# Four graph layers on one core: a mask and a product moved from VectorE to GpSimd, with other prices in the instruction planner

## The chip, the cores and the metric

The kernel runs on one core of one Trainium2 chip. The metric is the device time of one execution in microseconds (us); smaller is better. TensorE (PE in the profile; PEld is its weight load) multiplies matrices, VectorE (DVE) and ScalarE (ACT) work on tiles elementwise, GpSimd (POOL) can too, and SyncE (SP) issues most of the transfers (DMAs).

## The reference

There are 16 batches of 1024 nodes with 128 features, and for each batch a sparse adjacency matrix of 1024 x 1024. Four layers follow each other; each begins with a layer norm and a maximum with 0, and its result is added to its input.

```python
h = relu(layernorm(x)); x = x + L0(h, adj, adj, W, b)    # mean over neighbours, linear
h = relu(layernorm(x)); x = x + L1(h, adj, W, b)         # normalised adjacency, linear
h = relu(layernorm(x)); x = x + L2(h, adj, ...)          # two rounds of edge scores and messages
h = relu(layernorm(x)); x = x + L3(h, adj, W, a)         # attention
# L2, per round l: a score for each pair of nodes
hid    = relu(a[:, :, None, :] + b[:, None, :, :] + be1[l])
scores = sigmoid(hid @ We2[l] + be2[l])
messages = (adjacency * scores) @ x
# L3
e = (Wh1 + swapaxes(Wh2, 1, 2)) * A_                     # A_ = A + identity
e = where(e >= 0, e, ALPHA * e)
attention = softmax(where(A_ > 0, e, NEG_INF))
h_prime = attention @ Wh
```

## The kernel before, in words

The 1024 nodes of a batch are 8 blocks of 128. Layer 2 needs scores only where the adjacency matrix has an entry. For each pair of blocks the kernel builds one-hot matrices (`st`, `om`, `omT`, `onT`) from the matrix; matmuls with them pick the features of the two ends of each edge into slots (`pre`, L1343 and L1349), VectorE and ScalarE make the hidden values from them (`hid`, L1364 and L1365), and matmuls with a column of signs add them up to scores (L1389). Pairs of blocks are handled in nine groups: two of blocks on the diagonal, which have one direction, and seven off the diagonal, which have two directions, `d` 0 and 1. There are two rounds, `l` 0 and 1.

In `scores`, the scores of a group (`tan`) become `u`, two 16-bit halves in one 32-bit word (L1422, L1423; L1429 copies some rows to other partitions). Then `u` is multiplied with the one-hots `onT` into `val` (L1441): one instruction of 128 x 1024 for each direction of an off-diagonal group, two for a diagonal group. `scatter` spreads `val` over the matrix of the pair of blocks with matmuls (L1486). Those of direction 1 write only 64 rows of PSUM, since they use 64 columns of weights; they are called narrow below. The result is multiplied with the adjacency matrix (`upd`, L1493) and gives the messages (L439).

Layer 3 is in `Lane.layer3`. Its rows of output are taken in three parts (3, 3 and 2 blocks), and each part in four steps of two blocks `k`. A step loads a strip of the transposed adjacency matrix (`at`; it has one buffer, except in the last batch), adds the identity where it belongs (L764), makes the products `e` (L765, two instructions), the leaky maximum (L769), the exponential on ScalarE (L770), and multiplies by the mask "adjacency above 0" (L771: comparison and product in one instruction). Then TensorE adds up `e` times `wh` (the `hp` matmuls of L439). There are 12 steps in a batch, 192 in all.

GpSimd does only the powers of the layer norms (L496, eight in a batch, 128 in all) and a few set-up instructions.

Batches are interleaved: while layer 2 of one batch runs, layer 3 of the batch before and layers 0 and 1 of the next one, with the building of its one-hots, run beside it. Python generators first write down all instructions in a rough order (`weave`, with shares of time in `MAIN_US`, `FIRST_US`, `LAST_US`). Then the class `Issue` sets the order on every engine: it gives each instruction a price (`costs`), walks the graph of dependences forwards and backwards as a list scheduler with the number of buffers in mind (`walk`), and does so `PASSES` times; the plan with the earliest last start is written into the program as a fixed order for each engine's queue. So a price in `costs` changes no instruction, only the order. Every engine then works through its queue in that order, and an instruction that waits holds up what stands behind it.

The prices that matter below: `SWITCH_NS` is charged when TensorE goes from fp32 to 16-bit matmuls or from narrow to wide ones; a GpSimd instruction costs a flat 1560 ns.

Of the kernel before, what the change touches and what calls it, by code (L numbers as in the profile page):

```python
# [10 lines left out]
F32 = mybir.dt.float32  # L11
# [4 lines left out]
OP = mybir.AluOpType  # L16
# [41 lines left out]

SIGNAL_NS = 45.0
RESULT_NS = {"PE": 163.0, "Activation": 120.0, "DVE": 88.0, "Pool": 80.0}  # L60
SWITCH_NS = 60.0
DMA_NS, DMA_NS_PER_BYTE, DMA_NS_BEHIND, DMAS = 1900.0, 3.9e-3, 3.3e-3, 8
PASSES = 3


class Issue:
# [63 lines left out]
    def costs(self):  # L130


        self.busy, self.late, self.form, self.bytes = [], [], [], []
        for op, queue, kind in zip(self.ops, self.queue, self.kind):
            out, form = op.outs[0].bass_ap, (False, False)
            n, late, size = self.size(op.outs[0]), RESULT_NS.get(queue, 0.0), 0
            aps = [a.bass_ap for a in op.ins if hasattr(a, "bass_ap")]
            psum = bool(aps) and aps[0].space == bass.MemoryType.PSUM
            if kind == "Matmult":
                n = self.size(op.ins[0])  # L140
                form = op.ins[0].dtype == F32, out.shape[0] < 128
                if form[0]:
                    busy = max(n / 1.2 + 6, 112) * (1 if op.is_transpose else 2)
                else:
                    busy = 32 if form[1] else max(n / 2.4 + 2.5, 25)
            elif kind == "DMACopy":
                size = n * WIDTH[op.outs[0].dtype] * out.shape[0]
                inside = all(a.space == bass.MemoryType.SB for a in (out, aps[0]))
                busy = 630 if inside else 470
                late = DMA_NS + size * DMA_NS_PER_BYTE - busy  # L150
            elif queue == "Activation":
                busy = n / 1.2 + (50 if psum else 92) + 92 * (len(aps) - 1)
            elif queue == "DVE":
                wide = [a for a in aps if a.size() > 128]
                fast = kind == "TensorScalarPtr" and len(wide) == 1 and not psum
                if kind in ("BNStats", "TensorReduce"):
                    n = self.size(op.ins[0])
                busy = n * (0.53 if fast else 1.0625) + 55 + 64 * (len(aps) > len(wide))
            else:
                busy = 1560  # L160
            self.bytes.append(size)
            self.busy.append(busy)
            self.late.append(busy + late)
            self.form.append(form)
# [24 lines left out]

    def switched(self, j, was, back):  # L190
        one, two = (self.form[j], was) if back else (was, self.form[j])
        return any(a and not b for a, b in zip(one, two))

    def walk(self, rank, seq, back=False):


        n, queues = len(self.ops), sorted(set(self.queue))
        edges, others = (self.front, self.after) if back else (self.after, self.front)
        waits = [len(v) for v in others]
        users, turn, homes = self.turns(seq)  # L200
        given, parked, live, over = dict.fromkeys(homes, 0), {}, {}, {}
        ready, start, line = [0.0] * n, [0.0] * n, {q: [] for q in queues}
        soon, now = {q: [] for q in queues}, {q: [] for q in queues}
        free, sent, was = dict.fromkeys(queues, 0.0), [(0.0, 0.0, 0)] * DMAS, (False, False)

        def offer(j):

            new = {}
            for name in self.uses[j]:
                if name in turn and name not in live:  # L210
                    new.setdefault(self.tiles[name].tag, set()).add(turn[name])
                else:
                    ready[j] = max(ready[j], live.get(name, 0.0))
            for tag, mine in new.items():
                at = given[tag]
                while at in mine:
                    at += 1
                if at <= max(mine) or len(homes[tag]) < len(mine):
                    key = at + 1 if at <= max(mine) else given[tag]
                    parked.setdefault((tag, key), []).append(j)  # L220
                    return
                ready[j] = max(ready[j], sorted(homes[tag])[len(mine) - 1])
            heappush(soon[self.queue[j]], (ready[j], rank[j], j))

        for j in range(n):
            if not waits[j]:
                offer(j)
        for _ in range(n):
            at, q = min(
                (free[q] if now[q] else max(free[q], soon[q][0][0]), q)  # L230
                for q in queues if now[q] or soon[q]
            )
            while soon[q] and soon[q][0][0] <= at:
                heappush(now[q], heappop(soon[q])[1:])
            j = heappop(now[q])[1]
            more = 0.0
            if self.kind[j] == "DMACopy" and not back:
                at = max(at, sent[0][1])
                more = DMA_NS_BEHIND * sum(
                    n * (end - at) / (end - then) for then, end, n in sent if end > at  # L240
                )
                sent = sent[1:] + [(at, at + self.late[j] + more, self.bytes[j])]
            elif q == "PE":
                at += SWITCH_NS * self.switched(j, was, back)
                was = self.form[j]
            start[j], free[q] = at, at + self.busy[j]
            line[q].append(j)
            end = at + (self.busy[j] if back else self.late[j] + more + SIGNAL_NS)
            freed = {}
            for name in self.uses[j]:  # L250
                users[name] -= 1
                over[name] = max(over.get(name, 0.0), end)
                if name not in turn:
                    continue
                tag = self.tiles[name].tag
                if name not in live:
                    live[name] = heappop(homes[tag])
                    freed.setdefault(tag, []).append(given[tag] + 1)
                    given[tag] += 1
                if not users[name]:  # L260
                    heappush(homes[tag], over[name])
                    freed.setdefault(tag, []).append(given[tag])
            for tag, keys in freed.items():
                for key in dict.fromkeys(keys):
                    for k in parked.pop((tag, key), ()):
                        offer(k)
            for k, lag in edges[j]:
                ready[k] = max(ready[k], at + lag + more * (lag > 0.0))
                waits[k] -= 1
                if not waits[k]:  # L270
                    offer(k)
        return start, line
# [26 lines left out]
def tile_four_gnn_layers(  # L299
# [22 lines left out]
    nc = tc.nc  # L322
# [45 lines left out]
    rows = {name: const.tile([P, L, D], F32, name=f"{name}_bc") for name in ("gamma", "beta")}  # L368
# [362 lines left out]
    class Lane(Layers):  # L731
# [5 lines left out]
        def layer3(self, xt, strip, name):  # L737
# [14 lines left out]
            for lo, hi in L3_ROWS:  # L752
                n = hi - lo
# [3 lines left out]
                for k in range(0, T, 2):  # L757
                    at = strip(k, lo, hi)
                    e = flat(self.scratch(f"e_{name}_{lo}_{k}"))[:, : 2 * n * P]
                    e = e.rearrange("p (k n) -> p k n", k=2)  # L760
                    for i in range(2):
                        if lo <= k + i < hi:
                            own = at[:, i, (k + i - lo) * P : (k + i + 1 - lo) * P]
                            nc.vector.tensor_add(own, own, ident)  # L764
                        nc.vector.scalar_tensor_tensor(  # L765
                            e[:, i], wh1[:, lo * P : hi * P], wh2[:, k + i : k + i + 1], at[:, i],
                            op0=OP.add, op1=OP.mult,
                        )
                    nc.vector.scalar_tensor_tensor(e, e, L3_ALPHA, e, op0=OP.mult, op1=OP.max)  # L769
                    nc.scalar.activation(e, e, AF.Exp)  # L770
                    nc.vector.scalar_tensor_tensor(e, at, 0.0, e, op0=OP.is_gt, op1=OP.mult)  # L771
                    yield 0.4 * n
                    for i in range(2):
                        for t in range(n):
# [22 lines left out]
    class Edges:  # L797
# [490 lines left out]
        class Group:  # L1288
# [126 lines left out]
            def scores(self):  # L1415


                path, name, rows = self.path, self.name, self.rows
# [15 lines left out]
                for d in range(nd):  # L1434
                    for i in range(0, Q, each):
# [2 lines left out]
                        )  # L1438
                        n = val.shape[-1]
                        v = u[:, :, i * nd + d : (i + each - 1) * nd + d + 1 : nd]  # L1440
                        nc.vector.tensor_tensor(  # L1441
                            val, onT[:, i : i + each].rearrange("p i (c n) -> p i c n", n=n),
                            v.rearrange("p k i o -> p i k o").to_broadcast([P, each, SEGMENTS, n]),
                            op=OP.mult,
# [370 lines left out]
```

## Time and profile before

| what | value |
|---|---|
| time, median of 3 runs | 4691.72 us (4684.89 to 4700.5) |
| the profiled execution's own time | 4697.63 us |
| its span in the profile | 4695.5 us |
| mean granted TensorE clock | 0.979 |
| instructions | 132226 |
| GpSimd: powers of 128 x 8 (64), median | 1.637 us |
| GpSimd: powers of 128 x 4 (64), median | 1.007 us |
| VectorE: L765, 128 x 384 (256) and 128 x 256 (128), mean | 0.615 and 0.482 us |
| VectorE: L769, 128 x 768 (128) and 128 x 512 (64), mean | 0.956 and 0.686 us |

The profile is of one execution. Busy time is the time in which an engine had an instruction in work, as a share of the span; durations of VectorE instructions that follow each other overlap by a little under 0.1 us in the records. A group of instructions is shown as line, engine, operation, output<-input, shapes and count, then its busy time in us and the mean of one in ns, then the idle time of the engine just before them and who ended it. The chain of work is followed back from the last instruction, at each step to what released it. Idle time of an engine that isn't the bottleneck costs nothing.

### The profile page before, as it was taken

The page shows a single profiled execution, that of the slowest core. Times are in us where ns is not written, and L with a number is a line of the kernel's source. Part 1 is how long each engine was busy: PE and PEld are TensorE (multiplying, and loading weights), DVE is VectorE, ACT ScalarE, POOL GpSimd, SP SyncE. Part 2 cuts the span into 40 slices and gives each one's busy share as a digit, 9 for nine tenths or more (in the row PEclk, how much of TensorE's full clock was granted, in tenths as well). Part 3 has the DMA queues.
Part 4 walks back from the last instruction along what each step waited for, and adds up shares of the span by engine and source line. Part 5 has one row for each costly group of instructions (what it writes and reads, how often), then busy time and mean ns, then how long its engine had stood idle before and what let it go on. Part 6 is the DMA issues. An engine that isn't in the chain of part 4 may idle for free.

```text
span 4695.5 us, 132226 instructions
## 1 busy us (share of the span) xinstructions
PE 4427.7 (94%) x53685; PEld 3608.7 (77%) x53685; DVE 3876.9 (83%) x9128; ACT 3003.4 (64%) x7238; POOL 187.0 (4%) x137
## 2 busy tenths in 40 slices
PE   6999999999999999999999999999999999999986
PEld 5777778777777777877777787777877777787765
DVE  4777797987969789797897979879797897979877
ACT  5666575675756667576675766757567575766643
POOL 0000000000000000000000000000000000000000
PEclk8999999999999999999999999999999999999997
DMA  7363635345363443635436353453634426344221
GB/s 211 82 179 81 188 89 162 108 121 169 86 183 107 132 142 86 190 106 148 118 88 203 88 160 114 120 170 87 184 102 135 143 83 192 104 140 126 80 79 56
DMA packets 852858, 603.42 MB, mean 129 GB/s; under 512 B 128528, under 2 KB 782608, under 8 KB 852240
## 3 DMA queue, kind: packets, MB, share of 16 engines
q1 hardware_dynamic: 847136, 593.24, 43.4%
q8 instruction: 423, 6.93, 0.6%
q10 hardware_dynamic: 5104, 1.65, 0.1%
q14 instruction: 195, 1.60, 0.1%
HBM read 446.44 MB, written 100.66 MB: 117 GB/s over the span
## 4 chain that ended last, share of the span: by engine, by line
PE 54%; DVE 29%; ACT 7%; DMA 6%; issue 2%; POOL 1%; SPq 0%; ACTq 0%; DVEq 0%; POOLq 0%
PE nb L543 7%; PE pre L1343 7%; PE p L1486 7%; DVE hid L1365 6%; PE msg L439 5%; DVE val L1441 5%; PE sc L1389 4%; PE h L597 4%; PE pre L1349 4%; DVE omT L1197 2%; PE xn L606 2%; PE bb L551 2%; PE tn L1038 2%; DMA both<-part 2%; DVE upd L1493 2%
## 5 line engine op out<-in xcount | busy, mean ns | idle before, releaser
L1364 ACT ACTIVATE hid<-pre 128x320 f16<-128x320 f32 (+1 forms) x2048 | 903.5, 460 | 330.5 <-PE pre L1349 316.2
L1365 DVE SCALAR_TENSOR_TENSOR hid<-pre,hid 128x320 f16<-128x320 f32 (+1 forms) x2048 | 998.5, 508 | 97.2 <-ACT hid L1364 88.7
L1343 PE MATMUL pre<-om,part 128*128 128x320 fp8e4 (+1 forms) x4096 | 960.8, 308 | 14.3 <-DVE hid L1365 6.5
L1441 DVE TENSOR_TENSOR val<-onT,u 128x1024 f32<-128x1024 fp8e4 x576 | 695.9, 1218 | 1.8
L1349 PE MATMUL pre<-st,both 128*128 128x176 fp8e4 (+1 forms) x4096 | 678.1, 243 | 18.3 <-DMA both<-part 17.3
L439 PE MATMUL msg<-upd,xf 128*128 128x128 f32 (+3 forms) x3008 | 663.2, 329 | 1.9 <-DVE upd L1493 1.7
L1349 PEld LDWEIGHTS <-both 128*128 128x128 f16 x4096 | 385.5, 98 | 172.7 <-issue 27.5
L439 PEld LDWEIGHTS msg<-upd,xf 128*128 128x128 f32 x3008 | 428.7, 191 | 29.3 <-issue 13.6
L1389 PE MATMUL sc<-slide,hid 128*128 128x1 f16 x12800 | 438.6, 163 | 10.7 <-DVE hid L1365 10.0
L1389 PEld LDWEIGHTS <-hid 128*128 128x128 f16 x12800 | 408.2, 96 | 52.7 <-DVE hid L1365 25.3
L1204 ACT ACTIVATE om<-pm 128x320 fp8e4<-128x320 f32 (+1 forms) x576 | 271.6, 472 | 197.4 <-PE pm L1150 191.2
L1486 PE MATMUL p<-val,omT 128*128 128x64 f16 (+1 forms) x6528 | 383.0, 204 | 14.9 <-DVE val L1441 10.9
L1343 PEld LDWEIGHTS <-part 128*128 128x128 f16 x4096 | 339.6, 98 | 69.8 <-issue 30.1
L1410 ACT ACTIVATE tan<-sc,be_s,down 128x8 f32<-128x8 f32 (+1 forms) x960 | 297.9, 357 | 133.7 <-PE sc L1389 128.8
L1493 DVE SCALAR_TENSOR_TENSOR upd<-p,adj 128x512 f32<-128x512 f32 x512 | 351.5, 687 | 31.5 <-PE p L1486 25.6
L1486 PEld LDWEIGHTS <-omT 128*128 128x128 fp8e4 x6528 | 333.8, 97 | 41.0 <-issue 20.0
L439 PE MATMUL hp<-wh,e 128*128 128x129 f32 x2048 | 332.9, 289 | 23.7 <-DVE e L771 18.1
L1189 ACT ACTIVATE onT<-pn 128x256 fp8e4<-128x256 f32 (+1 forms) x576 | 253.1, 440 | 112.1 <-PE pn L1135 101.9
L439 PEld LDWEIGHTS hp<-wh,e 128*128 128x128 f32 x2048 | 275.4, 196 | 33.4 <-DVE e L771 21.9
L1110 ACT ACTIVATE far<-iota_off,mid 128x384 f16<-128x384 f16 x448 | 271.0, 628 | 44.6 <-DVE st L1114 42.8
L1114 DVE TENSOR_SCALAR st<-far,wid 128x384 fp8e4<-128x384 f16 (+1 forms) x576 | 238.9, 428 | 70.3 <-PE pre L1349 34.3
L543 PEld LDWEIGHTS nb<-z,l 128*128 128x128 f32 x2048 | 255.8, 196 | 27.0 <-issue 12.9
(224 smaller groups left out, 7943.9 us busy)
## 6 DMA issues: line engine op xcount, KB each, us to landing
at<-in_adj_dram SPq DMA_DIRECT2D x128, 512.0 KB, 5.1
ct<-in_adj_dram SPq DMA_DIRECT2D x128, 512.0 KB, 5.0
adjT<-tn SPq DMA_DIRECT2D x128, 512.0 KB, 6.1
l<-adjT SPq DMA_DIRECT2D x128, 512.0 KB, 5.1
adj<-adjT SPq DMA_DIRECT2D x256, 256.0 KB, 3.5
a<-adjT SPq DMA_DIRECT2D x128, 384.0 KB, 3.9
both<-part SPq DMA_DIRECT2D x256, 128.0 KB, 3.4
adj<-adjT SPq DMA_DIRECT2D x448, 64.0 KB, 2.6
```

The costliest lines, as they stand in the source:

```text
L439: nc.tensor.matmul(dst, left, right, start=opened is None, stop=True, skip_group_check=True)
L543: nc.tensor.matmul(ps, mat[:, k], z[:, k], start=(k == 0), stop=(k == T - 1))
L1204: nc.scalar.activation(om, pm, AF.Copy, saturate=False)
L1343: nc.tensor.matmul(pre[:, :c], parts[:, k, u % Q, 1 - d], om, start=(k == 0), stop=True, skip_group_check=True,)
L1349: ins = nc.tensor.matmul(pre[:, at : at + n], both[:, k, t % Q, d], st[:, first : first + n], start=False, stop=True, skip_group_check=True,)
L1364: nc.scalar.activation(hid[:, 0, :c], pre[:, :c], AF.Relu)
L1365: nc.vector.scalar_tensor_tensor(hid[:, 1, :c], pre[:, :c], 0.0, hid[:, 0, :c], op0=OP.max, op1=OP.subtract)
L1389: nc.tensor.matmul(sc[:, k, g : g + 1], self.hid[self.done + g][:, v, at : at + P], sign, start=(g, v, k) == (*order[0], 0), stop=True, sk ...
L1410: nc.scalar.activation(dst, src, AF.Tanh, bias=path.be2[:, self.l : self.l + 1], scale=path.down[:, self.l : self.l + 1],)
L1441: nc.vector.tensor_tensor(val, onT[:, i : i + each].rearrange("p i (c n) -> p i c n", n=n), v.rearrange("p k i o -> p i k o").to_broadcast ...
L1486: nc.tensor.matmul(dst, left, right, start=n < first, stop=True, skip_group_check=True)
L1493: nc.vector.scalar_tensor_tensor(upd, ps, S_SCALE, self.adj[:, d * Q : (d + 1) * Q], op0=OP.add, op1=OP.mult,)
```

## The change

Layer 3's mask is made on GpSimd in two instructions, a comparison that overwrites the strip and a product after the exponential, in place of VectorE's one. In round `l` 1, the product of scores and one-hots for direction 1 is issued on GpSimd. In the planner the prices change: a switch between narrow and wide matmuls costs 94 or 119 ns and one between fp32 and 16-bit none; a narrow matmul 29 ns; GpSimd instructions of 64 elements or more per row go by their length, and the flat price stays for the rest; VectorE instructions whose output begins at another partition than their input cost 130 ns more, and every small operand counts. There are four passes, not three.

```diff
-SWITCH_NS = 60.0
+NARROW_NS, WIDE_NS, HELD_NS = 94.0, 119.0, 130.0
-PASSES = 3
+PASSES = 4
...
-            out, form = op.outs[0].bass_ap, (False, False)
+            out, form = op.outs[0].bass_ap, False
...
-                form = op.ins[0].dtype == F32, out.shape[0] < 128
-                if form[0]:
+                form = out.shape[0] < 128
+                if op.ins[0].dtype == F32:
                     busy = max(n / 1.2 + 6, 112) * (1 if op.is_transpose else 2)
                 else:
-                    busy = 32 if form[1] else max(n / 2.4 + 2.5, 25)
+                    busy = 29 if form else max(n / 2.4 + 2.5, 25)
...
-                busy = n * (0.53 if fast else 1.0625) + 55 + 64 * (len(aps) > len(wide))
+                busy = n * (0.53 if fast else 1.0625) + 55 + 64 * (len(aps) - len(wide))
+                rows = {v[1] for v in map(self.span, (*op.ins[:1], *op.outs[:1])) if v}
+                busy += HELD_NS * (len(rows) > 1)
             else:
-                busy = 1560
+                busy = 1560 if n < 64 else (2.2 if len(aps) > 1 else 1.1) * n + 200
...
-        return any(a and not b for a, b in zip(one, two))
+        return 0.0 if one == two else NARROW_NS if two else WIDE_NS
...
-                at += SWITCH_NS * self.switched(j, was, back)
+                at += self.switched(j, was, back)
...
+                    nc.gpsimd.tensor_scalar(at, at, 0.0, None, op0=OP.is_gt)
                     nc.vector.scalar_tensor_tensor(e, e, L3_ALPHA, e, op0=OP.mult, op1=OP.max)
                     nc.scalar.activation(e, e, AF.Exp)
-                    nc.vector.scalar_tensor_tensor(e, at, 0.0, e, op0=OP.is_gt, op1=OP.mult)
+                    nc.gpsimd.tensor_tensor(e, e, at, op=OP.mult)
...
-                        nc.vector.tensor_tensor(
+                        by = nc.gpsimd if self.l and d else nc.vector
+                        by.tensor_tensor(
                             val, onT[:, i : i + each].rearrange("p i (c n) -> p i c n", n=n),
                             v.rearrange("p k i o -> p i k o").to_broadcast([P, each, SEGMENTS, n]),
                             op=OP.mult,
```

More of the change, by code (lines that the diff above doesn't have):

```diff
@@ L203, in walk @@
         soon, now = {q: [] for q in queues}, {q: [] for q in queues}
-        free, sent, was = dict.fromkeys(queues, 0.0), [(0.0, 0.0, 0)] * DMAS, (False, False)
+        free, sent, was = dict.fromkeys(queues, 0.0), [(0.0, 0.0, 0)] * DMAS, False
         def offer(j):
```

## The prediction, made before the changed kernel ran

> **What bounds the kernel now.** I read the page's busy table first. TensorE is in use nearly all the time and VectorE comes next; GpSimd does almost nothing. The chain of work that ended last alternates between the two busy engines.
>
> ```profile
> PE 4427.7 (94%) x53685; PEld 3608.7 (77%) x53685; DVE 3876.9 (83%) x9128; ACT 3003.4 (64%) x7238; POOL 187.0 (4%) x137
> ...
> PE 54%; DVE 29%; ACT 7%; DMA 6%; issue 2%; POOL 1%; SPq 0%; ACTq 0%; DVEq 0%; POOLq 0%
> ```
>
> A busy PE is not a PE at its peak, so I took the starts of successive matmuls of each form from the trace: the time between two starts, less the shortest usual one of that form, sums to about 870 us, of which some 115 us is a fixed cost (below). So PE waits for others for 600 to 700 us of 4695.5, and relief elsewhere can reach the end.
>
> Then busy time by stretches of 20 us over one batch (280 us). Columns: stretch, its length, PE, PEld, DVE, ACT, POOL busy us (instructions), granted clock, DMA share, GB/s.
>
> ```profile
> 900.00:920.00 20.00, 19.52 (x308) 15.98 (x306) 19.88 (x46) 15.54 (x47) 0.00 (x0) 1.00 0.17 47
> 920.00:940.00 20.00, 20.00 (x290) 16.77 (x289) 19.71 (x36) 11.71 (x29) 0.00 (x0) 1.00 0.31 84
> ...
> 1060.00:1080.00 20.00, 20.00 (x175) 15.67 (x175) 8.10 (x21) 10.08 (x17) 0.00 (x0) 1.00 0.89 266
> ```
>
> VectorE is full (18.6 us of 20 or more) in 7 of 14 stretches and slack in the rest. Of this batch's 12 L771 products, 8 fall in the full stretches between 860 and 960. I let 0.65 of any change in VectorE's load through to the end.
>
> The groups of instructions give the work that moves:
>
> ```profile
> L1441 DVE TENSOR_TENSOR val<-onT,u 128x1024 f32<-128x1024 fp8e4 x576 | 695.9, 1218 | 1.8
> ...
> L771 DVE SCALAR_TENSOR_TENSOR e<-a,e 128x768 f32<-128x768 f32 x128 | 122.0, 954 | 11.3 <-ACT e L770 11.1
> ...
> L771 DVE SCALAR_TENSOR_TENSOR e<-a,e 128x512 f32<-128x512 f32 x64 | 43.8, 684 | 0.1
> ```
>
> **What the Trainium skill says.** "SBUF — State Buffer", Who interferes with whom: VectorE and GpSimd share one pair of ports, held for a whole instruction; a VectorE instruction with two SBUF inputs, or in a two-port mode, and a GpSimd instruction that reads SBUF block each other, the later one fully. The trace shows one side of it. In the timeline (start, us, engine), a GpSimd power begins while such VectorE work runs:
>
> ```profile
> 746.88 1.09 DVE L1046 TENSOR_TENSOR has<-ct,tn 128x896 fp8e4<-128x896 f32 x1
> 747.08 2.38 POOL L496 TENSOR_TENSOR st<-st,half_neg 128x8 f32<-128x8 f32 x1 [14.77 <-DVE st L493]
> ...
> 4489.47 0.62 DVE L765 SCALAR_TENSOR_TENSOR e<-whr,whc,a 128x384 f32<-128x384 f32 x1
> 4489.63 3.32 POOL L496 TENSOR_TENSOR st_y<-st_y,half_neg 128x4 f32<-128x4 f32 x1 [21.15 <-DVE st_y L493]
> 4490.00 1.22 DVE L1441 TENSOR_TENSOR val<-onT,u 128x1024 f32<-128x1024 fp8e4 x1
> 4491.13 0.95 DVE L769 SCALAR_TENSOR_TENSOR e<-e 128x768 f32<-128x768 f32 x1
> ```
>
> The 128x8 power takes 1.637 us in the median, here 2.38, longer by about what was left of the 1.09 us instruction. The 128x4 one takes 1.007, here 3.32: it waited through three such instructions in a row. Starts inside L1365, which reads one operand from PSUM, never stretch it. The other side, VectorE held by GpSimd, no run here shows: a power reads 4 or 8 elements a row.
>
> "GPSIMD Engine Reference", Performance versus the Vector engine: a two-input fp32 tensor_tensor of 2048 took 4497 ns, so 2.2 ns an element; one input is cheaper, at 1.03 to 1.8 cycles. The trace has no streaming GpSimd instruction to compare. "TensorEngine Tiling (Array Packing)", Key Properties: a change of tiling mode drains TensorE. The trace agrees and gives the sizes: 94 ns into the 64-column matmuls of L1486, some 119 out of them. Going from fp32 to 16-bit matmuls costs 0 to 1 ns in the median.
>
> **The change part by part.** The sum is against the profiled execution's own time, 4697.6 us (span 4695.5), 5.9 above the median of 4691.7.
>
> 1. Off VectorE. Recorded durations overlap by about 0.09 us, so I use the time from start to start: 0.87 (768), 0.60 (512), 1.13 (val). L771 goes: 128 x 0.87 + 64 x 0.60 = 150 us. The product moves where l is 1 and d is 1: 7 off-diagonal groups x 16 batches = 112, x 1.13 = 126 us. Together 276 us less.
>
> 2. Onto GpSimd. By the page's price, an estimate: multiply 1.69 us (768) and 1.12 (512); val 2.25; the mask, at 1.4 cycles, 0.9 and 0.6. Sum 128 x 2.59 + 64 x 1.72 + 112 x 2.25 = 694 us; GpSimd goes from 187 to about 880 us busy, 19%, no bound by itself. fp8 and a broadcast input in val could cost more; up to twice is in the range.
>
> 3. The ports. These 496 instructions stream for their whole length. In the built program's order of VectorE I added up, after each L769 and each first-direction val of the second round, what is issued before the next instruction that needs the shared port (two SBUF inputs, or the two-port L1114). It is 1.1 to 1.4 us in the mean, often 0. A GpSimd instruction longer than this holds VectorE for the rest: in the mean 1.19 us for val, 0.69 and 0.50 for the multiply, 0.25 and 0.21 for the mask. 112 x 1.19 + 128 x 0.94 + 64 x 0.71 = 299 us back on VectorE. Ends: nothing (the lock is brief as with the powers) and 694 us (every one blocks fully). I take 299, for the page says the lock lasts. VectorE's net is 299 - 276 = +23 us; x 0.65 = +15.
>
> 4. The end of the last batch is layer 3 alone, with nothing else for VectorE:
>
> ```profile
> 4672.35 0.62 DVE L765 SCALAR_TENSOR_TENSOR e<-whr,whc,a 128x384 f32<-128x384 f32 x1
> 4672.88 0.69 DVE L769 SCALAR_TENSOR_TENSOR e<-e 128x512 f32<-128x512 f32 x1
> 4673.49 0.95 DVE L771 SCALAR_TENSOR_TENSOR e<-a,e 128x768 f32<-128x768 f32 x1
> 4674.35 0.96 DVE L769 SCALAR_TENSOR_TENSOR e<-e 128x768 f32<-128x768 f32 x1
> ```
>
> From 4647.9 to 4683.3 VectorE works almost without a gap, 35 us, all of it with two SBUF inputs. Afterwards it has 35 - 9 = 26, and GpSimd 8 x 2.59 + 4 x 1.72 = 28; they exclude each other, 54 in sum: +18 us. Without the lock about -3.
>
> 5. Waits. The multiply ends the path from exponential to the hp matmuls: 0.87 us becomes 1.69 plus a wait for the port. PE and its loads now wait 40 us for L771; I take that as doubled, +40, less half for time already counted in 3: +20. Queued behind the multiply, itself waiting for ACT's exponential, are the powers of the layer norms (VectorE's L503 and L619 wait for them) and the next val (PE's L1486 waits). The strip buffer is single, and stays taken until the multiply has ended, so SP's next load of it starts later, as do the loads behind it on SP's queue; VectorE waits 36 us for these loads now. For these +15. Ends 0 and +80.
>
> 6. The plan. All queues are laid out anew. The narrow runs on PE grow from 545 to 595 in the built order: 50 x 0.213 = +11 us. Dropping the charge on fp32-to-16-bit changes is right by the trace and lets the plan mix them freely; I can't price it: 0, with 40 us either way. HELD_NS, the 29 ns, the count of small operands and a fourth pass only alter this plan.
>
> Sum: 15 + 18 + 20 + 15 + 11 = +79; 4697.6 + 79 = 4777, less 5.9 for the median: 4771, say 4770.
>
> **The rivals.** A, faster: VectorE isn't held, as with the powers, or GpSimd's work falls beside L1365 and the PSUM readers, 2000 us of VectorE's time. Then 276 x 0.65 = 179 us goes, less 11 for switches and 35 for waits: 4697.6 - 133 - 5.9 = 4559; with half the stalls (150), about 4650. It decides below some 175 us of stall, where 0.65 x (276 - stall) covers the other 64 us. For it: VectorE's full stretches. Against it: the stretched powers. B, even: stalls near 175 us, 4692. C, much slower: val costs twice (112 x 2.25 = 252 us more on GpSimd, most of it lock); 0.65 x 252 = 164 more, 4930. Against it: the page's price per element knows nothing of fp8. That the change doesn't move the work is excluded by the built order, which has 496 more GpSimd instructions and 304 fewer on VectorE.
>
> **How the numbers follow.** Forecast (slower, 4720 to 4850) 0.52; A 0.33; B 0.09; C 0.06. A measurement tells about 0.3% (14 us) from no change. Faster 0.33, same 0.09, slower 0.58. The range runs from the middle of A, 4580, to the forecast's upper end, 4850; the forecast's own is 4720 to 4850.
>
> **What would show it.** Right: L765, L769 and the remaining L1441 grow longer or more spread on VectorE (medians 0.615, 0.957, 1.218 now) and VectorE stays above 3800 us busy; the tail from the first to the last e grows from 35 to over 50 us; PE waits more for POOL's e and val. Wrong: these durations unchanged and VectorE near 3600 us busy, which is A; or GpSimd's val above 3.5 us, which is C.

## The result and the profile after

The changed kernel takes 4844.98 us (median of 4 runs, 4837.08 to 4853.94) against 4689.94 for the kernel before: a ratio of 1.0328, with a 95% interval of 1.0299 to 1.0357. It is slower by 155 us, where the prediction said 78; the time lies inside the range, near its upper end.

Lines are numbered anew: L1441 of before is L1445, L765 is L767, L769 is L772, L771 has become L771 (the mask) and L774 (the product), L1486 is L1490, L1114 is L1117.

The same two lines of the page, of the kernel after:

```profile
PE 4427.6 (92%) x53685; PEld 3608.0 (75%) x53685; DVE 3918.7 (81%) x8824; ACT 3017.8 (62%) x7238; POOL 1143.0 (24%) x633
...
PE 30%; DVE 24%; issue 3%; ACT 3%; DMA 2%; POOL 1%; SPq 0%; DVEq 0%; ACTq 0%; POOLq 0%
```

VectorE has 304 instructions fewer and is busy for 42 us more. GpSimd hardly stands on the chain (1%), although the chain here is followed for only part of the span (the shares add up to 63%). So GpSimd isn't the bound; it makes another engine late. Which one, the groups of VectorE's instructions tell (count, then busy us and mean ns, then idle time before):

```profile
L1445 DVE TENSOR_TENSOR val<-onT,u 128x1024 f32<-128x1024 fp8e4 x464 | 696.2, 1504 | 3.1
...
L1117 DVE TENSOR_SCALAR st<-far,wid 128x384 fp8e4<-128x384 f16 x448 | 242.4, 558 | 29.1 <-ACT far L1113 26.4 <-PE pn L1138 1.2
L767 DVE SCALAR_TENSOR_TENSOR e<-whr,whc,a 128x384 f32<-128x384 f32 x256 | 160.9, 646 | 56.2 <-DMA a<-adjT 49.6 <-ACT whr L539 6.4
L772 DVE SCALAR_TENSOR_TENSOR e<-e 128x768 f32<-128x768 f32 x128 | 137.9, 1079 | 1.0
```

The 464 products that stay on VectorE are busy for 696.2 us, as long as the 576 of before (695.9): a mean of 1504 ns in place of 1218, with the median unchanged (1220) and the longest at 2946. L1117 went from 417 to 558 ns in the mean. Instructions that read an operand from PSUM keep their durations (`hid` of 320 columns: 484 now, 487 before). An instruction is called stretched below when it took longer than the shortest tenth of its form (same line, same shape) did. Summed over VectorE, this excess is 370 us, against 49 before; 314 us of it lies in instructions during which GpSimd was at work. These 314 us are the stalls.

GpSimd's own groups:

```profile
L771 POOL TENSOR_SCALAR a<-a 128x768 f32<-128x768 f32 (+1 forms) x192 | 408.0, 2125 | 1068.1 <-DVE e L767 683.9 <-issue 74.8 <-PE pre L1352 60.2
L774 POOL TENSOR_TENSOR e<-e,a 128x768 f32<-128x768 f32 (+1 forms) x192 | 321.3, 1674 | 159.5 <-issue 79.4 <-POOL a L771 38.9 <-ACT e L773 34.3
L1445 POOL TENSOR_TENSOR val<-onT,u 128x1024 f32<-128x1024 fp8e4 x112 | 231.2, 2064 | 263.3 <-DVE u L1432 90.1 <-PE pre L1352 52.3 <-ACT hid L1367 45.8
```

And a stretch of the timeline (start us, duration us, engine) in which a product of each engine becomes ready from the same `u`:

```profile
1215.12 1.57 DVE L1432 COPY u<-u 64x16 f16<-64x16 f16 x1
1216.72 0.49 DVE L1368 SCALAR_TENSOR_TENSOR hid<-pre,hid 128x320 f16<-128x320 f32 x1
1216.83 1.92 POOL L1445 TENSOR_TENSOR val<-onT,u 128x1024 f32<-128x1024 fp8e4 x1 [0.17 <-DVE u L1432]
1217.13 2.71 DVE L1445 TENSOR_TENSOR val<-onT,u 128x1024 f32<-128x1024 fp8e4 x1
...
1219.89 0.48 PE L1490 MATMUL p<-val,omT 128*128 128x128 f16 x9 [1.28 <-DVE val L1445]
```

VectorE has one `hid` ahead in its queue; GpSimd has nothing, and starts. VectorE's product of direction 0 starts 0.3 us later and ends at 1219.84, 1.09 us after GpSimd's. Alone it needs 1.22 us, so it was held until 0.13 us before GpSimd's recorded end. PE waits for it. The copy above it, which takes 0.17 us alone, was held in the same way by the GpSimd instruction before, a multiply.

GpSimd doesn't always hold VectorE for as long as its own instruction lasts. A mask, and the leaky maximum behind it (start us, duration us, engine):

```profile
625.88 2.13 POOL L771 TENSOR_SCALAR a<-a 128x768 f32<-128x768 f32 x1 [5.93 <-DVE e L767]
626.24 1.27 DVE L772 SCALAR_TENSOR_TENSOR e<-e 128x768 f32<-128x768 f32 x1
```

L772 needs 0.95 us alone and ends at 627.51, so it was held until 0.68 us after the mask's start, not for the mask's 2.13 us. The prediction had, from the Trainium skill, the ports held for a whole instruction; for the mask's reads the trace says otherwise, and throughout. Where the 768-wide mask itself had its usual length and no other GpSimd instruction came in, 33 of the L772 began in its first 0.65 us, and 32 of them were stretched, released 0.69 us after its start in the median; 32 began later in the mask, and none was stretched by more than 0.02 us. L1117, in a two-port mode, was held longer: eight were released only some 1.93 us after the mask's start. As for the other two GpSimd instructions, the multiply holds VectorE for 1.66 of its 1.81 us and val for 1.79 of its 1.92, by median.

### The profile page after: what moved, and what is told of

Its sections match the earlier page's. It is cut to its first block, busy times and chain, and to the rows that moved or that the text cites. A ratio compares the mean times of both kernels' runs of the same rounds, so it can differ in the third digit from the quotient of the medians.

```text
span 4835.3 us, 133096 instructions
## 1 busy us (share of the span) xinstructions
PE 4427.6 (92%) x53685; PEld 3608.0 (75%) x53685; DVE 3918.7 (81%) x8824; ACT 3017.8 (62%) x7238; POOL 1143.0 (24%) x633
## 4 chain that ended last, share of the span: by engine, by line
PE 30%; DVE 24%; issue 3%; ACT 3%; DMA 2%; POOL 1%; SPq 0%; DVEq 0%; ACTq 0%; POOLq 0%
DVE hid L1368 5%; PE pre L1346 4%; PE p L1490 4%; DVE val L1445 4%; PE nb L545 3%; PE msg L441 3%; DVE st L1117 3%; PE h L599 3%; PE sc L1392 2%; PE pre L1352 2%; DVE upd L1497 2%; DVE e L767 2%; DVE omT L1200 1%; PE xn L608 1%; DVE e L772 1%
## 5 line engine op out<-in xcount | busy, mean ns | idle before, releaser
L1346 PE MATMUL pre<-om,part 128*128 128x320 fp8e4 (+1 forms) x4096 | 983.3, 312 | 37.1 <-DVE hid L1368 31.5
L1445 DVE TENSOR_TENSOR val<-onT,u 128x1024 f32<-128x1024 fp8e4 x464 | 696.2, 1504 | 3.1
L771 POOL TENSOR_SCALAR a<-a 128x768 f32<-128x768 f32 (+1 forms) x192 | 408.0, 2125 | 1068.1 <-DVE e L767 683.9
L441 PE MATMUL msg<-upd,xf 128*128 128x128 f32 (+3 forms) x3008 | 646.4, 329 | 3.6 <-DVE upd L1497 3.4
L1490 PE MATMUL p<-val,omT 128*128 128x64 f16 (+1 forms) x6528 | 376.8, 205 | 100.4 <-DVE val L1445 93.5
L498 POOL TENSOR_TENSOR st_y<-st_y,half_neg 128x4 f32<-128x4 f32 x64 | 72.9, 1139 | 1571.3 <-DVE st_y L495 862.6
L1490 PEld LDWEIGHTS <-omT 128*128 128x128 fp8e4 x6528 | 335.3, 97 | 124.5 <-issue 110.6
L1497 DVE SCALAR_TENSOR_TENSOR upd<-p,adj 128x512 f32<-128x512 f32 x512 | 350.5, 685 | 41.7 <-PE p L1490 35.4
L441 PE MATMUL hp<-wh,e 128*128 128x129 f32 x2048 | 351.2, 293 | 29.2 <-POOL e L774 29.2
L774 POOL TENSOR_TENSOR e<-e,a 128x768 f32<-128x768 f32 (+1 forms) x192 | 321.3, 1674 | 159.5 <-issue 79.4
L1117 DVE TENSOR_SCALAR st<-far,wid 128x384 fp8e4<-128x384 f16 (+1 forms) x576 | 318.7, 572 | 36.1 <-ACT far L1113 32.5
```

The source lines that it names most:

```text
L441: nc.tensor.matmul(dst, left, right, start=opened is None, stop=True, skip_group_check=True)
L771: nc.gpsimd.tensor_scalar(at, at, 0.0, None, op0=OP.is_gt)
L774: nc.gpsimd.tensor_tensor(e, e, at, op=OP.mult)
L1117: nc.vector.tensor_scalar(on, far[:, :n], s.wid[:, i : i + 1], None, op0=OP.is_le, saturate=False)
L1346: nc.tensor.matmul(pre[:, :c], parts[:, k, u % Q, 1 - d], om, start=(k == 0), stop=True, skip_group_check=True,)
L1445: by.tensor_tensor(val, onT[:, i : i + each].rearrange("p i (c n) -> p i c n", n=n), v.rearrange("p k i o -> p i k o").to_broadcast([P, ea ...
```

## The experiments

Each ratio is to the kernel before on the same chip. Twelve kernels ran, in three groups on three chips, beside which the kernel before took 4690, 4684 and 4683 us; a difference between kernels of different groups is therefore uncertain by some 7 us, beside what follows.

**How much does an order alone move the time?**

```diff
 # kernel before
-SIGNAL_NS = 45.0
+SIGNAL_NS = 46.0
```

> The kernel before with one price of the planner moved by a nanosecond (the signal from 45 to 46 ns), as a measure of how much a new order alone moves the time. Both theories: the same work in a slightly different order, within 15 us of before. If it moves by 50 us or more, differences of that size between re-planned kernels can't be put down to an edit.

Measured: 4653.87 us, 0.9926 (0.9907 to 0.9946). All theories missed: the same work, planned with a price one nanosecond off, is 36 us faster. So no single pair of re-planned kernels tells less than some 40 us apart (by the last pair below, some 60), and the following needs larger effects, or pairs that agree.

**The planner alone, and each move alone**

```diff
 # e1_plan_only: changed kernel, both moves undone; e2_mask_only and e3_val_only undo one
-                    nc.gpsimd.tensor_scalar(at, at, 0.0, None, op0=OP.is_gt)
-                    nc.gpsimd.tensor_tensor(e, e, at, op=OP.mult)
+                    nc.vector.scalar_tensor_tensor(e, at, 0.0, e, op0=OP.is_gt, op1=OP.mult)
...
-                        by = nc.gpsimd if self.l and d else nc.vector
-                        by.tensor_tensor(
+                        nc.vector.tensor_tensor(
```

> The changed planner with all work back on VectorE. Theory 1 (the shared port and the waits for GpSimd cost the time): within 40 us of before, some 4700 us. Theory 2 (the new prices and the order they make cost most of it): about 4790 us, 100 us slower than before. GpSimd busy about 187 us and no stretched VectorE instructions in both.

Measured: 4643.97 us, 0.9907 (0.9888 to 0.9927): 46 us faster than before, a little outside what theory 1 had, and on the other side of theory 2, which falls. GpSimd's work therefore costs not 155 us but about 201.

> The changed planner, the mask's two instructions on GpSimd, the product back on VectorE. Theory 1: VectorE is rid of 150 us and gets about 175 us of stalls, the last 12 steps take about 48 us and not 35, and hp waits for GpSimd: 50 to 90 us slower than the planner alone. Theory 2: within 20 us of the planner alone.

Measured: 4727.5 us, 1.0082 (1.0061 to 1.0104), 84 us slower than the planner alone; 156 us of stretched VectorE instructions. The last 12 steps, from the first `e` to the last `hp` matmul, take 51.0 us and not 37.6.

> The changed planner, only the second direction's product of round 1 on GpSimd. Theory 1: VectorE is rid of 126 us and gets about 138 us of stalls; the matmuls of L1490 wait longer: 30 to 70 us slower than the planner alone, the tail of the last batch as before (35 us). Theory 2: within 20 us of the planner alone.

Measured: 4709.02 us, 1.0049 (1.003 to 1.0068), 65 us slower than the planner alone; the tail is as before (38.5 us). Of the 112 GpSimd products 110 held VectorE for more than 0.1 us, all of them together for 154 us, which is 1.38 us each: more than the 1.13 us that each saved. Both kernels are as theory 1 had them. The 65 us alone would be little more than the luck of an order.

**The moves under the old planner**

```diff
 # kernel before, with the two moves and no other change
+                    nc.gpsimd.tensor_scalar(at, at, 0.0, None, op0=OP.is_gt)
...
-                    nc.vector.scalar_tensor_tensor(e, at, 0.0, e, op0=OP.is_gt, op1=OP.mult)
+                    nc.gpsimd.tensor_tensor(e, e, at, op=OP.mult)
...
+                        by = nc.gpsimd if self.l and d else nc.vector
```

> The two moves to GpSimd with the planner of before (its old prices, a flat 1560 ns for every GpSimd instruction, three passes). Theory 1 (port and waits): the moves cost what they cost under the new planner, about 200 us, so 4840 to 4940, with some 300 us of stretched VectorE instructions. Theory 2 (it is the new planner together with the moves, which orders for GpSimd times that aren't met): the flat price does no worse than the new ones, 4750 or less.

Measured: 4922.85 us, 1.0507 (1.0484 to 1.0531), with 306 us of stretched instructions. The moves cost 238 us under the old prices and 201 under the new ones: it isn't the new planner that spoils them.

**Relief without GpSimd, and GpSimd without reading**

```diff
 # e7_left_out: changed kernel, both GpSimd instructions of the mask gone, and
+                        if self.l and d:
+                            for h in range(each):
+                                self.val[d, i + h] = self.val[0, i + h]
+                            continue
```

> The changed planner with the moved work left out on all engines: no mask is applied in layer 3, and in round 1 direction 1 uses direction 0's product. This is VectorE's relief of 276 us without port and without waits for GpSimd. Theory 1: VectorE near 3600 us busy and 0.65 of the relief at the end, 180 us under the planner alone: 4440 to 4540. Theory 2 (VectorE doesn't bound, PE and its waits do): within 60 us of the planner alone, 4580 to 4640.

Measured: 4540.42 us, 0.9695 (0.9669 to 0.9721). This kernel leaves the moved work out, so its output is of no use. The time stands at the very edge of theory 1's range (4540), and theory 1's share of 0.65 missed. The busy lines of the planner alone and of this kernel, one after the other:

```profile
PE 4365.7 (94%) x53685; PEld 3588.1 (77%) x53685; DVE 3872.0 (83%) x9128; ACT 2992.1 (64%) x7238; POOL 194.5 (4%) x137
```

```profile
PE 4341.3 (96%) x53685; PEld 3568.4 (79%) x53685; DVE 3612.3 (80%) x8824; ACT 2997.7 (66%) x7238; POOL 186.9 (4%) x137
```

VectorE is rid of 260 us and the end comes 104 us earlier: a share of 0.40 (0.38 of the 276 us that were counted off), give or take 0.15 for the luck of an order.

```diff
 # e8_write_only: changed kernel, each moved instruction becomes two fills
-                    nc.gpsimd.tensor_scalar(at, at, 0.0, None, op0=OP.is_gt)
+                    for _ in range(2):
+                        nc.gpsimd.memset(at, 1.0)
```

> As the changed kernel, but each moved GpSimd instruction is replaced by two fills with ones of the same tile, so GpSimd writes as long and at the same places in the graph of dependences but reads nothing from SBUF; mask and product are not computed. Theory 1 (VectorE is held by GpSimd's reads): val, L767 and L772 keep their medians, only the two-port L1117 may still be stretched; VectorE under 3700 us busy; 4480 to 4640. Rival (the slower and later results of GpSimd cost it, not the port): near the changed kernel, 4780 to 4850.

Measured: 4553.85 us, 0.9725 (0.9706 to 0.9745). The mask and the moved products are left out here too. The rival falls by some 230 us. VectorE's groups in this kernel:

```profile
L1452 DVE TENSOR_TENSOR val<-onT,u 128x1024 f32<-128x1024 fp8e4 x464 | 561.6, 1215 | 1.7
...
L1119 DVE TENSOR_SCALAR st<-far,wid 128x384 fp8e4<-128x384 f16 x448 | 223.0, 509 | 26.8 <-ACT far L1115 23.6 <-PE pre L1354 1.5 <-ACT hid L1369 0.5
L767 DVE SCALAR_TENSOR_TENSOR e<-whr,whc,a 128x384 f32<-128x384 f32 x256 | 148.8, 609 | 16.3 <-DMA a<-adjT 7.6 <-ACT whr L539 5.8 <-PE hp L441 2.4
L773 DVE SCALAR_TENSOR_TENSOR e<-e 128x768 f32<-128x768 f32 x128 | 121.4, 949 | 0.9
```

GpSimd is busy for 923 us, and the fills for mask and multiply stand at the same places in the graph of dependences as what they replace. The fills for val don't: they read no `u`, so they need not wait for it, as GpSimd's products do for 90 us in the changed kernel. A late val from GpSimd therefore isn't tested here; in the trace of the changed kernel PE waits 0.8 us in all for one, so it isn't what costs. GpSimd only writes here, and the instructions with two SBUF inputs are as short as before (val 1215, not 1504). Only instructions in a two-port mode are still held (L1119 at 509; 73 us in all). This is what the Trainium skill, "SBUF — State Buffer", Who interferes with whom, says: a second SBUF input of VectorE contends with GpSimd's reads, not with writes. One reserve: the fills for mask and multiply, at 2 x 0.75 us, are 0.6 and 0.3 us shorter than what they stand for; those for val, 2 x 0.98, are as long. And 13 us over the kernel without any of it is within the luck of an order.

**Can the twin be spared?** (The twin is VectorE's product of direction 0 in the group whose direction 1 GpSimd computes.)

```diff
 # e9_twin_first: changed kernel
+                        if self.l and d:
+                            nc.vector.tensor_copy(val[:, 0, 0, :1], self.val[0, 0][:, 0, :1])
                         by.tensor_tensor(
```

> As the changed kernel, with a one-column copy on VectorE from direction 0's product into direction 1's tile, so that GpSimd's product can't start before VectorE's product of the same group has ended. Theory 1a (GpSimd takes the port first, and what it holds is mostly the twin product on VectorE, for which PE then waits): the stall caused by GpSimd's products falls from 138 to under 60 us and PE's wait for val from 94 to under 40; 40 to 90 us faster than the changed kernel, 4750 to 4805. Rival (any other VectorE instruction with two SBUF inputs is hit instead, as the order counted, 1.1 us each): the stall stays above 100 us and the time within 30 us of the changed kernel.

Measured: 4853.52 us, 1.0355 (1.0327 to 1.0383), the same as the changed kernel; the 112 added copies take VectorE 16 us, too little to hide a gain of 40 to 90. Theory 1a falls. The wait of PE for val did go, from 94 to 23 us, and VectorE's products have their old length again:

```profile
L1449 DVE TENSOR_TENSOR val<-onT,u 128x1024 f32<-128x1024 fp8e4 x464 | 568.6, 1232 | 2.9
...
L1117 DVE TENSOR_SCALAR st<-far,wid 128x384 fp8e4<-128x384 f16 x448 | 299.1, 684 | 27.8 <-ACT far L1113 26.2
```

But GpSimd's products still hold VectorE for 124 us (138 in the changed kernel): the next instruction in need of the port is hit instead, L1117 above all, at 684 ns in place of 417.

**Foreseen and unforeseen time**

The stalls are 314 us and the relief 260, yet the sum cost 201 us. Theory P: the fixed order takes up what it foresees and passes on what it doesn't.

```diff
 # e10_hidden: planner alone, all work on VectorE
+            if queue == "DVE" and (mask or ...):   # the 304 instructions of the two moves
+                busy = 1.0
```

> The changed planner with all work on VectorE (as the planner alone), but the planner is told that the 304 instructions of the mask and of round 1's second product take 1 ns. Same work, nothing on GpSimd, no stall; only the order doesn't know of 276 us of VectorE's time. Theory P (VectorE's time that the fixed order doesn't foresee reaches the end in full, time that it foresees by 0.4): 4540 + 276, some 4760 to 4860. Rival (foreseen or not makes no difference; a stall costs by its place, behind GpSimd): as the planner alone, 4600 to 4690.

Measured: 4761.33 us, 1.0167 (1.015 to 1.0184), 117 us slower than the planner alone with the same work and the same engines, VectorE busy for 3882 us. Over the kernel without this work it is 221 us for 276, a share of 0.8, at the lower edge of theory P; the rival falls. In this one order, time that the plan doesn't know costs about twice what time that it knows costs; the 117 us are nearly twice the most that a nudge of a price moved.

```diff
 # e11_port_plan: changed kernel, measured GpSimd prices, and in walk
+            if self.port[j]:
+                at = max(at, port)
+                port = at + self.busy[j]
             start[j], free[q] = at, at + self.busy[j]
```

> The changed kernel with the shared port in the planner: in its walk an instruction of VectorE with two SBUF inputs or one in a two-port mode, and a GpSimd instruction of 64 or more elements a row, can't overlap; GpSimd's prices are those measured (2.53 n + 190 ns for the mask, 2.1 n + 200 for two inputs). Theory P: the stalls stay, some 200 to 300 us, but are foreseen, and 0.4 of them reaches the end: 4640 to 4740. Rival (a stall costs the same, foreseen or not): 4800 to 4880.

Measured: 4970.02 us, 1.0614 (1.0596 to 1.0631): a miss on both sides, and the slowest of all. 347 us of instructions are still stretched, and VectorE and PE wait for each other more than in the changed kernel (VectorE's L1209 for PE 189 us against 81, PE's `hp` for GpSimd 68 against 29). The granted TensorE clock is the lowest of all kernels, 0.955. So putting the port into the plan in this simple way doesn't mend the matter, and theory P isn't shown by this side.

**The luck of an order, once more**

> The changed kernel with the planner's signal at 46 ns: another order of the same work. All theories: within 40 us of the changed kernel, 4805 to 4885. Outside it the 155 us is in part the luck of one order.

Measured: 4783.15 us, 1.0218 (1.02 to 1.0236), 62 us under the changed kernel (52 by the two ratios), outside what was expected; 268 us of stretched instructions. As the expectation says, part of the 155 us is then the luck of one order: the same work in this order is 100 us slower than the kernel before.

> The planner alone (all work on VectorE) with the signal at 46 ns. All theories: within 40 us of 4644, 4604 to 4684. Outside it the new prices' gain over before is the luck of one order.

Measured: 4607.49 us, 0.985 (0.9829 to 0.9871), within what was expected and the fastest of the kernels that do all the work; it beats the kernel before and the changed one.

The pairs agree where it matters. New prices without moves: 46 us faster than the old ones at 45 ns (4644 against 4690) and at 46 ns (4607 against 4654). The moves: 201 us slower at 45 ns, 176 at 46 ns and, under the old prices, 238. So it stands on three pairs that the moves cost some 200 us, give or take the luck of an order.

## Why the prediction was right, and where it was off

Its direction, its time's range and its main mechanism, GpSimd's reads holding VectorE, held; its sum came out at half. Two things in that are luck. The 155 us belong to one order, and in the other one that was tried the same work cost 100, so some 50 to 60 of the 76 us by which the sum fell short may be no more than that. And the sum would have been further off without a second error: the moves alone (steps 3, 4 and 5) were put at +68 and cost 176 to 238, while the new prices (step 6) were put at +11 and gained 46. By its steps:

1. *Off VectorE, 276 us.* Right: 260 by the busy lines. What it is worth was set at 0.65 and measured at 0.40.
2. *Onto GpSimd, 694 us.* Too little: 956. The multiply (1.81 us in the median, 1.69 foreseen) and val (1.92 against 2.25) were near; the mask took 2.13 and 1.49 us where 0.9 and 0.6 were assumed, since one input was taken, from the skill's page, to be cheaper; here it is dearer. As GpSimd doesn't bind, the error itself cost little outside the tail. That the mask's stalls came to 45 us, as foreseen, is luck: it was too short in the sum, but it was also taken to hold VectorE for its whole length, and it holds most of it for its first 0.69 us only (0.47 for 512 columns).
3. *The ports, 299 us back on VectorE.* Right, and nearly by kind: 314, of which val 138 (133 foreseen), multiply 130 (120), mask 45 (45). Who is hit was not seen: mostly the twin product. The kernel that lets the twin go first shows that the sum doesn't hang on that. The step that failed stands at its end: "VectorE's net is 299 - 276 = +23 us; x 0.65 = +15". The net was right (+42 in the busy lines), but relief and stall don't pass to the end by the same share. Relief gave 104 us; from the kernel without the work to the changed one, 314 us of stalls with all that follows cost 305, and from the write-only kernel, 241 us of stalls cost 291. Counted so, the step is some +188 to +201 (tail and waits within), not +15 (with tail and waits, +68). The cause of the difference is shown in part, by one order: it passed on unforeseen time at 0.8, foreseen at 0.4. Why stalls come to 1.0 or more stays open.

   One part of it is on record, the granted TensorE clock. Between the first 150 us and the last 80 it stands at half in 32 stretches of the changed kernel, 164 us together, and in 10 stretches, 41 us together, of the kernel without the work. In the 7 us before each of the 32, TensorE was busy for 0.43 to 0.76 of the time, 0.67 in the mean, against 0.93 over this whole part: the half clock follows its waits. Before the one shown here, VectorE's copy and product had been held as in the stretch above (1.58 us in place of 0.17, 2.70 in place of 1.22); columns as in the prediction:

```profile
2972.25:2979.25 7.00, 4.20 (x40) 3.35 (x38) 6.94 (x9) 5.20 (x14) 4.59 (x3) 1.00 0.30 81
2979.25:2986.08 6.83, 6.66 (x71) 5.83 (x70) 4.19 (x11) 3.19 (x10) 0.00 (x0) 0.50 0.14 42
```

   At half clock a `pre` matmul of 320 columns starts every 266 ns and not every 136. Half of the 123 us more at half clock, some 60 us, is an estimate of the most that this adds to the 305 us; the kernel whose order doesn't foresee the work (0.8) has it too, with 140 us at half clock. What else raises the share, no run shows.
4. *The tail, +18.* Near in size, by another path: from the first `e` to the last product 48.3 us in place of 35.4, +13. The share of each engine in that stretch (PE, PEld, DVE, ACT, POOL busy us):

```profile
4775.00:4824.00 49.00, 25.77 (x133) 22.74 (x132) 38.80 (x46) 12.32 (x21) 46.92 (x24) 0.62 0.15 46
```

   GpSimd works almost without a gap, 46.9 of 49 us, and its 24 instructions alone, at their median lengths, are 43 us (an estimate: 8 x (2.13 + 1.81) + 4 x (1.49 + 1.27)): the tail is as long as GpSimd's own work. The prediction had 28 us of it, and 54 as the sum of two engines that exclude each other; they overlap, VectorE being busy, in part held, for 38.8 us. That the sum came near is luck. Before, VectorE was busy for 32.2 of 37 us with a product more per step.
5. *Waits, +35.* Not shown as a cost of its own. What waits for the results of the mask and the multiply on GpSimd, without reads, is within 13 us (the write-only kernel). PE waits for VectorE instead, here before and after:

```profile
PE p L1486 <- DVE val L1441: 10.9, 31, 2.8
...
PE p L1490 <- DVE val L1445: 93.5, 88, 2.1
...
PE hp L441 <- POOL e L774: 29.2, 16, 10.8
```

   The wait for val belongs to step 3; the one for the multiply was 18.1 us before, for VectorE's L771.
6. *The plan, +11 with 40 either way.* The narrow runs did grow, but the new prices gain 46 us in both pairs, just outside.

Put together from measured parts: 4690 - 46 (plan) - 104 (relief) + 305 (stalls, tail and waits) = 4845. The parts are differences along one chain of kernels, so they add up whatever their cause. Rival A had relief of 179 us and no stalls. Its premise is refuted by VectorE's stretched instructions, which the write-only kernel is free of but for the two-port ones; and even where it holds the time is 4540 to 4554 us, near its 4559 only because the new plan helped. (Its 4650 for half the stalls doesn't come out of its own terms: 0.65 x (276 - 150) - 64 = 18 us gained, some 4674.) Rival C's price for val (twice) was refuted: 1.92 us.

## What to carry to other kernels

Moving work from a nearly full VectorE to an idle GpSimd was no relief here, where both work from SBUF: count, in VectorE's queue, how soon after each GpSimd instruction the next one with two SBUF inputs or in a two-port mode comes, and set the held time against the saved time, instruction by instruction. Take the held time from a trace: it can be far shorter than the GpSimd instruction. Don't net the two before asking what each is worth: in the one order that tested it, time that the plan didn't foresee reached the end at twice the share of time that it did. Where the order is planned, change a price by a trifle and measure, to learn how much of a result is luck, before reading a cause into it.

## What the runs showed of the hardware that was not expected

A one-input comparison on GpSimd takes longer than a two-input multiply of the same size: 2.13 against 1.81 us for 768 elements a row, 1.49 against 1.27 for 512, by median. Yet it holds VectorE's instructions with two SBUF inputs only for its first 0.69 us, and two-port ones for some 1.93. The product with an fp8 input and a broadcast one is the cheapest of the three per element, 1.92 us for 1024. A fill of 768 takes 0.75 us. GpSimd's writes alone still hold VectorE's two-port instructions, for 73 us in the write-only kernel. Stretches of half TensorE clock follow TensorE's waits: 164 us of them in the changed kernel, 41 in the one without the work. And one nanosecond in a planner's price moved the time by 36, 37 and 62 us in three pairs of kernels, 0.8 to 1.3% (the last two across groups; by their ratios 27 and 52).
